# One part of a shared expert's inner layer moved behind the routed experts, and every fetch of their results paced

## The chip, the cores and the metric

The kernel runs on one core of a Trainium2 chip. The metric is the device time of one execution in microseconds (us). PE is the matrix engine (TensorE), DVE the vector engine, ACT the scalar engine with its function tables, POOL the general engine (GpSimd), which here issues the indirect DMAs, and SP the engine that issues most plain DMAs. Lines are written L1367 and so on.

## The reference, cut to what matters

Two blocks with a residual connection each. The first is a two-layer GRU over 1024 tokens of two sequences, and takes some two thirds of the time; the change leaves it alone. The second is a mixture of experts over the 2048 tokens:

```
xf = x.reshape(-1, 256)                                  # 2048 tokens
shared = silu(xf @ w1) * (xf @ w3) @ w2                  # inner width 512
s = sigmoid(concat([xf, t_emb]) @ router_W)              # 8 experts
topk_idx = top_k(s + router_bias, 2)
combine[n, e] = the two chosen s, divided by their sum
h = gelu(einsum('nc,ech->enh', xf, W1e))                 # inner width 256
y = einsum('enh,ehc->enc', h, W2e)
routed = einsum('ne,enc->nc', combine, y)
out = x + (shared + routed) / 3
```

## The kernel before, in words

All is float32. After the GRU the tokens stand in `x1`, 256 features on partitions, and once more by token in `base` and in the DRAM tensor `given`. The function `moe` then does the following.

*Routing.* DVE works out the two experts of each token, their shares, and a sorted order in which each block of 128 slots belongs to one expert. Its product is `pick` (L1179): for each of 39 blocks the tokens to gather. It also makes `words`, the experts' numbers packed eight to a word, which PE's sequencer loads into registers (`owner_of`, L1260), and `slots`, where each token's two results will lie.

*The shared expert's inner layer.* It is cut into 16 parts: four blocks of 512 tokens by four slices of 128 inner features. A part is two accumulated products (`hidden_sums`, L969: w1 into one PSUM bank, w3 into another, each of two 128x512 products; a float32 product shows as two matmul instructions in the profile), a sigmoid on ACT into the buffer `sig` (L981), and two multiplies on DVE, first into `silu` (L982), then into the hidden store (L983). `sig` and `silu` have two buffers each. One part is made before `moe`. Of the other 15, in `parts`, the first `EARLY` are made beside the routing, the next one (up to `FILL`) is spread through the end of the expert loop, and the rest come behind the experts. With EARLY = 8 these are 8, 1 and 6.

*The experts.* `go_through` handles 35 blocks always and up to 4 more under a branch (L1320). A block: POOL gathers 128 token rows from `given` with an indirect DMA (`fetch`, L1274), PE transposes them and DVE copies them (`xT`, L1237 and L1239), PE multiplies by the expert's first weights (`ps_h`, L1245), ACT applies gelu, then transposes, second weights, and a write of y to the DRAM tensor `back` (L1291). Fetches run three blocks ahead.

*Behind the experts.* A part with an order written out by hand, so that each engine gets its instructions just as the Python runs. POOL fetches each token tile's two results from `back` (`fetch_back`, L1335), 32 fetches in all, and DVE adds each times its share onto `base` (`add_gone`, L1349). The first eight fetches (BACK) are issued at once. Then the remaining parts of the inner layer follow, with two fetches behind each part, and then 16 output tiles j with one fetch each while any are left: four accumulated products with w2 into `ps_s` (L1367), an add onto `base` (L1375), and the write of the result from ACT's queue (L1376).

A fetch is paced by a one-element copy on POOL (L1334) from a tile that other work makes to the place that the fetch will fill: the copy can't run before that tile is there, and the fetch can't run before the copy. In the parts the tiles are `sig` and `silu`, in the output tiles `base` of tile j - 1. Before the change, fetches with an even number are paced and those with an odd number follow freely. A PSUM bank comes from one ring of seven (`bank`), so a product waits until DVE or ACT has read what stood in its bank seven allocations earlier.

Of the kernel before, what the change touches and what calls it, by code (L numbers as in the profile page):

```python
# [67 lines left out]

BACK = 8

EARLY = 8
FILL = EARLY + 1


# [935 lines left out]
def moe(ctx, tc, tag, front, out):  # L1010
# [213 lines left out]
    def shared_hidden(parts):  # L1224
        for blk, m in parts:
            pa, pb = (front.hidden_sums(bank, blk, m, name)[0] for name in ("w1", "w3"))
            made = [wk.tile([P, TB], FP, name=name) for name in ("sig", "silu")]
            front.hidden(blk, m, pa, pb, *made)
        return made

    shared_hidden(parts[:EARLY])

# [73 lines left out]

    ((blk, m),) = parts[EARLY:FILL]
    sums = []
# [19 lines left out]
    def fetch_back(behind=None):  # L1328
        i = len(gone)
        if i == 2 * NT:  # L1330
            return
        yb = rows[:, AWAY + i % (ROWS - AWAY), :]
        if behind is not None and i % 2 == 0:
            nc.gpsimd.tensor_copy(yb[0:1, 0:1], behind[0:1, 0:1])  # L1334
        nc.gpsimd.indirect_dma_start(  # L1335
            out=yb,
            out_offset=None,
            in_=back[:, :],
            in_offset=bass.IndirectOffsetOnAxis(ap=slots[:, i % 2, i // 2 : i // 2 + 1], axis=0),
        )  # L1340
        gone.append(yb)
# [14 lines left out]
    with tc.manual_schedule():  # L1356
        for _ in range(BACK):
            fetch_back()
        for i, part in enumerate(parts[FILL:]):
            for made in shared_hidden([part]):  # L1360
                fetch_back(made)
            add_gone(i - 1)
        for j in range(NT):
            fetch_back(base[:, j - 1, :] if j else None)
            ps = bank("ps_s")[:, 0:D]
            for k in range(KS):
                nc.tensor.matmul(  # L1367
                    out=ps,
                    lhsT=front.hid(k, slice(j * P, (j + 1) * P)),
                    rhs=w2_sb[:, k, :],  # L1370
                    start=(k == 0),
                    stop=(k == KS - 1),
                )
            add_gone(min(len(parts[FILL:]) - 1 + j, NT // 2 + j // 2))
            nc.vector.scalar_tensor_tensor(base[:, j, :], ps, 1.0 / 3.0, base[:, j, :], ALU.mult, ALU.add)  # L1375
            nc.scalar.dma_start(out=out[j * P : (j + 1) * P, :], in_=base[:, j, :])  # L1376
# [74 lines left out]
```

## Time and profile before

| | |
|---|---|
| median of three runs | 531.96 us (531.33 to 532.04) |
| the profiled execution | 538.56 us, of it a span of 536.8 us |
| PE busy | 512.1 us, 95% of the span |
| DVE busy | 385.1 us, 72% |
| ACT busy | 243.6 us, 45% |
| POOL busy | 76.9 us, 14% |
| ps_w, 8 early parts and their neighbours | ends at 395.4 us |
| experts | 395.4 to 475 us |
| 6 parts behind the experts | 476.1 to 496.8 us |
| 16 output tiles | 496.8 to 531.2 us |

A row of a timeline gives the start and the duration in us, the engine, the line, the operation, the output and its inputs, how many instructions are merged, and in brackets how long the engine had been idle and what released it. "issue" means that the profile shows nothing that the engine waited for. A row of a line's view gives the shortest, median and longest duration in ns and the first and last start in us; PEldq is PE's sequencer, which runs ahead of the matrix array.

### The profile page before, as it was taken

The page shows a single profiled execution, that of the slowest core. Times are in us where ns is not written, and L with a number is a line of the kernel's source. Part 1 is how long each engine was busy: PE and PEld are TensorE (multiplying, and loading weights), DVE is VectorE, ACT ScalarE, POOL GpSimd, SP SyncE. Part 2 cuts the span into 40 slices and gives each one's busy share as a digit, 9 for nine tenths or more (in the row PEclk, how much of TensorE's full clock was granted, in tenths as well). Part 3 has the DMA queues.
Part 4 walks back from the last instruction along what each step waited for, and adds up shares of the span by engine and source line. Part 5 has one row for each costly group of instructions (what it writes and reads, how often), then busy time and mean ns, then how long its engine had stood idle before and what let it go on. Part 6 is the DMA issues. An engine that isn't in the chain of part 4 may idle for free. (4 is left out here: it accounts for less than half of the span.)

```text
span 536.8 us, 18511 instructions
## 1 busy us (share of the span) xinstructions
PE 512.1 (95%) x7492; PEld 341.2 (64%) x7492; DVE 385.1 (72%) x1296; ACT 243.6 (45%) x833; POOL 76.9 (14%) x124
## 2 busy tenths in 40 slices
PE   7999999999999999999999999989999999999795
PEld 4556766666665545665665666654458888854584
DVE  3665789999888888888888888888953333336372
ACT  3444355655665656656666565641133333341000
POOL 1200000000000000000000000002064444037570
PEclk9999999999999999999999999999999999999888
DMA  8980000000000000000000000001024443223252
GB/s 283 373 259 2 2 3 4 3 4 2 4 32 3 12 1 4 2 23 22 3 23 2 23 22 4 22 21 61 1 88 128 120 125 123 70 72 104 81 177 85
DMA packets 23103, 32.13 MB, mean 60 GB/s; under 512 B 3056, under 2 KB 18544, under 8 KB 22992
## 3 DMA queue, kind: packets, MB, share of 16 engines
q1 hardware_dynamic: 17344, 19.94, 11.0%
q0 software_dynamic: 3216, 8.79, 5.8%
q10 hardware_dynamic: 2448, 2.11, 1.2%
q8 instruction: 63, 1.03, 0.8%
q14 instruction: 32, 0.26, 0.2%
HBM read 21.26 MB, written 9.57 MB: 57 GB/s over the span
## 5 line engine op out<-in xcount | busy, mean ns | idle before, releaser
L296 PE MATMUL ps_step<-whh_sb,h 128*32 128x192 f32 x3616 | 193.3, 331 | 5.4 <-DVE h L369 4.2
L296 PEld LDWEIGHTS ps_step<-whh_sb,h 128*32 128x32 f32 x3616 | 94.6, 109 | 71.4 <-DVE h L369 51.9
L360 DVE TENSOR_TENSOR_SCAN row<-gates,n 128x128 f32<-128x128 f32 x230 | 98.0, 426 | 29.6 <-ACT n L355 28.3
L344 DVE TENSOR_TENSOR_SCAN ps_step<-gates,ps_step 128x128 f32<-128x128 f32 x230 | 97.3, 423 | 15.0 <-ACT gates L341 15.0
L268 PE MATMUL ps_step<-wih_sb,h 128*32 128x192 f32 x1696 | 99.7, 328 | 4.1 <-ACT ps_step L526 2.4
L355 ACT ACTIVATE n<-ps_step 128x64 f32<-128x64 f32 x228 | 53.0, 232 | 111.0 <-DVE ps_step L344 110.9
L341 ACT ACTIVATE gates<-ps_step 128x128 f32<-128x128 f32 x230 | 66.5, 289 | 35.5 <-PE ps_step L296 26.0
L268 PEld LDWEIGHTS ps_step<-wih_sb,h 128*32 128x32 f32 x1696 | 57.4, 110 | 26.8 <-ACT ps_step L526 14.5
L369 DVE STREAM_TRANSPOSE h<-row 128x64 f32<-128x64 f32 x230 | 56.5, 246 | 8.0
L969 PE MATMUL ps_w<-x_sb,w_sb 128*128 128x512 f32 x128 | 57.3, 597 | 0.2 <-PEq L1320 0.2
L268 PE MATMUL ps_in<-wih_sb,h 128*32 128x192 f32 x1024 | 54.4, 328 | 1.8 <-ACT h L257 1.4
L1239 DVE COPY hT<-ps_hT 128x256 f32<-128x256 f32 x35 | 14.9, 425 | 49.0 <-PE ps_hT L1237 47.1
L526 ACT COPY ps_step<-inputs 128x256 f32<-128x256 f32 x123 | 47.8, 389 | 0.0
L357 DVE SCALAR_TENSOR_TENSOR n<-gates,row 128x64 f32<-128x64 f32 x224 | 47.0, 210 | 0.0
L268 PEld LDWEIGHTS ps_in<-wih_sb,h 128*32 128x32 f32 x1024 | 34.0, 110 | 14.6 <-issue 4.6
L526 ACT COPY ps_step<-bt 128x256 f32<-128x256 f32 x106 | 39.9, 376 | 3.3
L1274 POOL DMA_INDIRECT inputs<-given,pick x35 | 33.3, 951 | 55.2 <-PE ps_xT L1237 31.9
L969 PEld LDWEIGHTS ps_w<-x_sb,w_sb 128*128 128x128 f32 x128 | 23.6, 190 | 27.1 <-issue 24.7
L1245 PE MATMUL ps_h<-w1e_sb,xT 128*128 x140 | 36.1, 380 | 0.7 <-DVE xT L1239 0.7
L1245 PE MATMUL ps_y<-w2e_sb,hT 128*128 x140 | 36.0, 380 | 0.0
L1335 POOL DMA_INDIRECT inputs<-back,slots x32 | 30.9, 964 | 30.0 <-issue 28.3
L1245 PEld LDWEIGHTS ps_y<-w2e_sb,hT 128*128 128x128 f32 x140 | 26.4, 190 | 4.8 <-DVE hT L1239 1.3
(179 smaller groups left out, 430.9 us busy)
## 6 DMA issues: line engine op xcount, KB each, us to landing
back<-y SPq DMA_DIRECT2D x35, 128.0 KB
w1e_sb<-in_w1e SPq DMA_DIRECT2D x1, 2048.0 KB
w2e_sb<-in_w2e SPq DMA_DIRECT2D x1, 2048.0 KB
given<-inputs SPq DMA_DIRECT2D x8, 256.0 KB
out_dram<-inputs ACTq DMA_DIRECT2D x16, 128.0 KB
whh_sb<-in_whh SPq DMA_DIRECT2D x2, 768.0 KB
x_sb<-in_xT SPq DMA_DIRECT2D x3, 512.0 KB
w_sb<-in_w SPq DMA_DIRECT2D x3, 512.0 KB
```

Source lines behind the costliest of these rows:

```text
L268: last = nc.tensor.matmul(out=out[cols(q), :, :], lhsT=given(k), rhs=self.wih[layer][:, k, q * 3 * U : (q + 1) * 3 * U].rearrange("p (g u) ...
L296: nc.tensor.matmul(out=by_sum(self.sums[layer])[cols(q), 0:3, :], lhsT=self.states[layer][:, k, :], rhs=self.whh[layer][:, k, q * 3 * U : ...
L341: nc.scalar.activation(gates[:, :, :, 1], sums[:, 1:3, :], AF.Sigmoid)
L344: nc.vector.tensor_tensor_scan(s, gates[:, 0, :, :].rearrange("p u i -> p (u i)"), ps[:, 0 : 6 * U : 3], 0.0, ALU.mult, ALU.add,)
L355: nc.scalar.activation(n[:, :, 0], s[:, 1 : 2 * U : 2], AF.Tanh, scale=-1.0 if keep is None else keep)
L357: nc.vector.scalar_tensor_tensor(n[:, :, 1], gates[:, 1, :, 1], 1.0, h, ALU.subtract, ALU.mult)
L360: nc.vector.tensor_tensor_scan(row.rearrange("p u i -> p (u i)"), gates[:, 1, :, :].rearrange("p u i -> p (u i)"), n.rearrange("p u i -> p ...
L369: nc.vector.transpose(to, row)
L526: return nc.scalar.copy(by_sum(banks[layer][tick % 2])[:, 0:4, :], g.sum_bias[1] if layer else inputs[:, group_of(0, tick), :, :],)
L969: last = self.tc.nc.tensor.matmul(out=ps, lhsT=self.later[name][:, k, m * P : (m + 1) * P], rhs=self.x1[:, k, blk * TB : (blk + 1) * TB], ...
L1245: nc.tensor.matmul(out=ps, lhsT=of[:, k, :], rhs=weights_sb[:, bass.ds(e * KD + k, 1), :], start=(k == 0), stop=(k == KD - 1),)
L1274: nc.gpsimd.indirect_dma_start(out=xg, out_offset=None, in_=given[:, :], in_offset=bass.IndirectOffsetOnAxis(ap=pick[:, i : i + 1], axis=0),)
```

## The change

EARLY goes from 8 to 7. So 7 parts are made beside the routing, the part in the expert loop's end is the eighth of `parts` (block 2, slice 0) and no longer the ninth (block 2, slice 1), and 7 parts come behind the experts. With two fetches behind each, 22 of the 32 fetches are issued before the output tiles and not 20. In `fetch_back` the condition on even numbers is gone, so that every fetch is paced that is given a tile: 14 in the parts and 9 in the output tiles.

```
-EARLY = 8
+EARLY = 7
 FILL = EARLY + 1
...
         yb = rows[:, AWAY + i % (ROWS - AWAY), :]
-        if behind is not None and i % 2 == 0:
+        if behind is not None:
             nc.gpsimd.tensor_copy(yb[0:1, 0:1], behind[0:1, 0:1])
         nc.gpsimd.indirect_dma_start(
             out=yb,
```

More of the change, by code (lines that the diff above doesn't have):

```diff
@@ L69 @@
 BACK = 8
-EARLY = 8
+EARLY = 7
 FILL = EARLY + 1
@@ L1332, in fetch_back @@
         yb = rows[:, AWAY + i % (ROWS - AWAY), :]
-        if behind is not None and i % 2 == 0:
+        if behind is not None:
             nc.gpsimd.tensor_copy(yb[0:1, 0:1], behind[0:1, 0:1])
```

## Prediction

> **What bounds the kernel now.** I read the page first (busy shares, the chain that ended last), then the timeline of PE, POOL, ACT and DVE from 360 us on, then PE's sequencer at the lines where the experts begin. All times are of the one profiled execution.
>
> ```profile
> PE 512.1 (95%) x7492; PEld 341.2 (64%) x7492; DVE 385.1 (72%) x1296; ACT 243.6 (45%) x833; POOL 76.9 (14%) x124
> PE ps_s L1367 6%; PE ps_w L969 4%; DVE inputs L1375 0%
> ```
> PE is the bound, and from 476 us to the end its own instructions are the chain. The change leaves the first 365 us alone (the recurrent layers, L296 and L268).
>
> Where the experts begin, PE's timeline:
> ```profile
> 387.61 7.97 PE L969 MATMUL ps_w<-x_sb,w_sb 128*128 128x512 f32 x18
> 395.42 0.60 PE L1237 MATMUL ps_xT<-ident,inputs 128*128 128x128 f32 x4
> 396.70 1.13 PE L1245 MATMUL ps_h<-w1e_sb,xT 128*128 x4 [0.68 <-DVE xT L1239]
> ```
> A part of the inner layer is 8 of these matmuls. The 18 are the tail of the sixth early part, the seventh and the eighth; the eighth is the one that moves. PE looks full right up to the first expert, so one would think that all of its time comes back. The sequencer's instructions say otherwise:
> ```profile
> L1237 PEldq EVENT_SEMAPHORE  x2: 51/51/51, 392.6 to 392.9; - x2
> L1260 PEldq TENSOR_LOAD <-words x1: 493/493/493, 393.5 to 393.5; - x1
> L1245 PEldq EVENT_SEMAPHORE  x1: 51/51/51, 394.3 to 394.3; - x1
> ```
> The waits for the first two gathers pass at 392.6 and 392.9, then the experts' numbers are loaded at 393.5, and the first expert's product is ready to go out at 394.35. This is hidden now because the matrix array has queued work until 395.4.
>
> POOL, at the two places where it gathers:
> ```profile
> 388.55 1.18 POOL L1274 DMA_INDIRECT inputs<-given,pick  x1 [19.99 <-DVE pick L1179]
> 390.03 0.94 POOL L1274 DMA_INDIRECT inputs<-given,pick  x1 [0.31 <-issue]
> ...
> 487.36 0.18 POOL L1334 COPY inputs<-sig 1x1 f32<-1x1 f32 x1
> 487.80 0.97 POOL L1335 DMA_INDIRECT inputs<-back,slots  x1 [0.27 <-POOL inputs L1334]
> 489.08 0.95 POOL L1335 DMA_INDIRECT inputs<-back,slots  x1 [0.30 <-issue]
> 490.04 0.18 POOL L1334 COPY inputs<-sig 1x1 f32<-1x1 f32 x1
> ...
> 510.38 0.36 POOL L1334 COPY inputs<-inputs 1x1 f32<-1x1 f32 x1 [3.87 <-DVE inputs L1375]
> 511.08 1.00 POOL L1335 DMA_INDIRECT inputs<-back,slots  x1 [0.33 <-POOL inputs L1334]
> ```
> A pair with one copy takes 490.04 - 487.36 = 2.68 us, an unpaced fetch 1.25 us, so a paced one 1.43 us. POOL never waits here before 506 us.
>
> The chain of waits at the end:
> ```profile
> 476.11 20.84 PE ps_w L969 x48
> 496.95 6.26 PE ps_s L1367 x29
> 503.21 0.46 issue
> ...
> 507.90 23.23 PE ps_s L1367 x94
> ```
> Six parts take 20.7 us (3.44 each). The 128 products of ps_s begin at 496.79 and at their steady 0.216 us would take 27.6 us, to 524.4; they end at 531.1. So 6.7 us are lost between 503 and 514, to gaps that no instruction explains and then to half clock. The execution took 538.56 us, 6.60 over the median of 531.96. I read this stall as that one execution's and not the timed runs' (an estimate, from 6.7 against 6.6). The sum below is a difference and is put on both.
>
> **The change part by part.**
> *Taken from the front:* 8 weight loads and 8 matmuls (8 x 0.43 = 3.44 us of PE), one sigmoid on ACT (0.60), two multiplies on DVE (2 x 0.69), no DMA. PE then ends the seventh part at 391.99 instead of 395.42. But the first gather starts only when DVE has made `pick` (388.25), which the change does not hasten. So the transposes go out at 392.65 and 393.05; DVE, free at 392.88, copies the first until 393.55; and the sequencer, having passed the second gather's wait at 392.95, still takes its 1.4 us to 394.35 for the load of the experts' numbers. The first product starts at about 394.45 instead of 396.69: 2.24 us earlier, not 3.44. Behind it gathers keep ahead of their use (the sixth starts at 395.03, freed by the earlier transposes, and is wanted near 401), and the gelu table load on ACT comes 3.4 us earlier too.
>
> *A rule against the row.* The first gather took 392.6 - 388.55 = 4.05 us from its issue, the second 2.9. The Trainium skill, "DMA: Bandwidth & Descriptors", section "Anatomy of one DMA — SWDGE (gpsimd) path", gives about 2.0 us plus bytes over 436 GB/s, so 2.3 us for 128 KB. By the rule the gather lands at 390.85, the sequencer has its numbers before PE is free, and the front gives back all 3.44: sum 0. By the row it gives 2.24. I take the row.
>
> *Added behind:* the same 3.44 us of PE after the branch at L1320, where PE has no gap to take it: +3.44. Nothing of SP's or POOL's queue comes with it, apart from two fetches that now run in the part loop and not in the output loop. The part in the middle of the experts' end (FILL) becomes (2,0) instead of (2,1), the same work.
>
> *Pacing:* copies go from 11 to 23, each 0.18 us and its hand-over, 1.43 - 1.25 = 0.18 us of POOL: 2.1 us on POOL in all. Queued behind each copy are all later fetches. New too: a silu buffer (two of them) is free only when POOL has copied from it, so DVE's multiply two parts on waits for POOL, with L983 and the adds behind it. Counted from the first part's first matmul (POOL's first fetch is at +1.54, as 477.65 - 476.11): the eight free fetches end at 11.25, the copies then come every 1.43; those of parts 3 and 4 end at 20.0 to 24.3, and let parts 5 and 6 be finished on DVE at 22.8 and 25.6. PE wants the bank of the last part again at 34.5 (ps_s tile 6), so it does not wait. The last fetch ends at 11.25 + 23 x 1.43 + 1.25 = 45.4; with 2.0 to land and 1.0 for two adds, 48.4, and the last add stands before the output multiply of tile 14, whose sums are ready at 24.1 + 15 x 1.73 = 50.0. Hidden, with 1.6 us to spare; the cover is PE's 27.6 us of ps_s.
>
> Sum: -2.24 + 3.44 + 0 = +1.20 us. On the median: 533.2. On the profiled execution: 539.8 with the stall, 533.1 without.
>
> *A second rule, against the change.* From 392.0 to 394.45 PE would have only four transposes. The Trainium skill, "TensorE: Matmul & The Clock Gate", section "Part 1: The HAM clock gate (the "warmup" mystery)", has the clock halved after an idle window of about 3.4 us; an opening of 2.4 us would then cost nothing. This trace is stricter: the clock went to half at 506.66 after a stretch of 3.4 us in which PE still ran five matmuls of 0.216 us, 32% of it. The worst stretch of that length at the front would hold about 0.4 us of the seventh part, 0.44 of transposes and 0.55 of ps_h, 40%. Half clock cost 2.8 us there (14 matmuls in 5.79 us instead of 3.02). By the rule the sum stays +1.20, by the row it could be +4.0. I take 0, since 40% is over 32%, and keep 2.8 as the high end.
>
> **The rivals.**
> *A. No change (531.9 to 532.5).* The gather lands sooner in the timed runs, or the number load overlaps more. For it: the rule above, and the array's queue is full in the profile. Against: both waits passed exactly as the gathers' traffic ended (DMA share 0.73 at 392.0 to 392.4). It decides if the first product starts before 393.8, 0.6 us sooner than I say.
>
> *B. POOL becomes the bound (534.0 to 537.8).* The limit for a paced fetch is (50.0 - 15.5)/23 = 1.50 us. Two copies behind DVE's output cost 0.70 us to the fetch (510.38 to 511.08), not 0.44. If the nine in the output loop do, 2.4 us come, less 1.6 to spare: +2.0 in all. If all 23 do, 6.2 - 1.6 + 1.2 = +5.8. Against: later copies of that loop took 0.18 again.
>
> *C. Faster (525 to 531).* If the stall at 503 us is in the timed runs too and fetches cause it, spacing them ends it: up to -6.7 + 1.2 = -5.5. Against: POOL issues without pause in both, so 1.43 instead of 1.34 us a fetch is hardly thinner traffic, and the 6.6 us argue that the timed runs lack it. It decides if over 2.3 us of a real stall go.
>
> **How the numbers follow.** The three runs lie within 0.13%, so about 0.2% (1.06 us) can be told from no change. Likeliest, 0.58: 533.2, own range 532.6 to 533.9; of it 0.44 lies beyond 1.06 us and 0.14 within. A has 0.09, B 0.13, the half clock (536.0) 0.07, C 0.13. So slower 0.44 + 0.13 + 0.07 = 0.64, same 0.14 + 0.09 = 0.23, faster 0.13. The range 530.5 to 536.3 leaves out most of C and the far end of B.
>
> **What would show it.** Right: PE's last ps_w before the experts ends near 392.0; xT at 392.7; first ps_h near 394.4 with some 2 us of idle around it; 56 ps_w after the branch; copies of sig and silu 14, of base 9; the part loop 24 us without PE gaps. Wrong: ps_h before 393.8 (A); the last L1375 waiting for a fetch, or paced fetches over 1.5 us apart (B); ps_s without gaps in the timed runs, and a gain (C).

## The result and the profile after

The changed kernel took 532.47 us in the median (532.05 to 534.17, 14 runs), the kernel before 531.59 us (14 runs). The ratio of the means is 1.0022, with a 95% interval of 1.0013 to 1.0030: 1.2 us slower (0.7 to 1.6), where the sum said +1.20. The medians lie 0.9 us apart. The profiled execution took 532.48 us, of it a span of 530.7.

The page after, busy shares:

```profile
PE 509.8 (96%) x7492; PEld 340.6 (64%) x7492; DVE 385.2 (73%) x1296; ACT 243.5 (46%) x833; POOL 79.5 (15%) x136
```
POOL has its twelve copies more (136 instructions, not 124). That PE's busy time is 2.3 us lower than on the page before is no gain of the change: the half clock of that first execution is missing from it.

PE's timeline where the experts begin, and below it PE's sequencer at the same place (shortest, median, longest in ns, then first and last start in us):

```profile
387.09 4.54 PE L969 MATMUL ps_w<-x_sb,w_sb 128*128 128x512 f32 x10
392.18 0.77 PE L1237 MATMUL ps_xT<-ident,inputs 128*128 128x128 f32 x4 [0.55 <-DMA inputs<-given,pick]
393.91 1.10 PE L1245 MATMUL ps_h<-w1e_sb,xT 128*128 x4 [0.96 <-DVE xT L1239]
```
```profile
L1237 PEldq EVENT_SEMAPHORE  x2: 51/51/51, 392.1 to 392.4; - x2
L1260 PEldq TENSOR_LOAD <-words x1: 492/492/492, 393.0 to 393.0; - x1
L1245 PEldq EVENT_SEMAPHORE  x1: 51/51/51, 393.8 to 393.8; - x1
```
Everything stands 0.52 us earlier in this trace, `pick` at 387.54, so times are best counted from `pick`. The seventh part now ends first, PE waits for the gather and then once more, and ps_h starts at pick + 6.37. Before it was pick + 8.63. The bracket blames DVE's copy of xT for the second wait. But DVE copied the two blocks' xT from 392.62 to 393.41, and the first block's copy, the only one that this product needs, was done well ahead of 393.91. What ended just before ps_h is the load of the experts' numbers and what the sequencer does behind it.

The chain of waits at the end:

```profile
473.10 24.27 PE ps_w L969 x56
497.37 27.64 PE ps_s L1367 x128
525.01 0.02 issue
525.04 0.42 DVE inputs L1375
```
Seven parts now take 24.27 us, and ps_s takes the 27.6 us that it should. No stall is there.

A second profile of the unchanged kernel:

> The kernel before, unchanged, for a second profile. My theory: the 6.7 us lost between 503 and 514 us in the first profile were that execution's own, so here the 128 products of ps_s take 27.6 us without a break, the last output add comes about 136.4 us behind the pick, and the span is near 530 us. Rival (the stall belongs to the kernel): ps_s takes some 34 us again and the span is near 537 us.

It took 531.41 us with a span of 529.6. Its chain:

```profile
475.62 20.84 PE ps_w L969 x48
496.46 27.64 PE ps_s L1367 x128
524.10 0.02 issue
524.12 0.42 DVE inputs L1375
```
The stall was the first execution's own. With this trace (`pick` at 387.77, ps_h at pick + 8.62) the whole difference can be counted from `pick` to the last output add, which comes at +136.35 before and at +137.50 after: ps_h comes 2.25 us sooner; from there to the first part behind the experts 79.22 and 79.19 us go by, so 0.03 sooner; the parts take 24.27 in place of 20.84, so 3.43 later; ps_s takes the same. That is 1.15 us later in all.

### The profile page after: what moved, and what is told of

It is laid out like the page before. It is cut to its first block, busy times and chain, and to the rows that moved or that the text cites. A ratio compares the mean times of both kernels' runs of the same rounds, so it can differ in the third digit from the quotient of the medians.

```text
span 530.7 us, 18536 instructions
## 1 busy us (share of the span) xinstructions
PE 509.8 (96%) x7492; PEld 340.6 (64%) x7492; DVE 385.2 (73%) x1296; ACT 243.5 (46%) x833; POOL 79.5 (15%) x136
## 5 line engine op out<-in xcount | busy, mean ns | idle before, releaser
L1285 ACT ACTIVATE he<-ps_h 128x256 f32<-128x256 f32 x35 | 13.4, 383 | 35.3 <-PE ps_h L1245 35.3
```

## The experiments

**Only the part moved.** On the kernel before, pacing as it was:

```
-EARLY = 8
+EARLY = 7
```


> EARLY = 7 with fetches paced as before (every second one). My theory: the move alone costs what the change costs, because PE gets 3.44 us more behind the experts and only some 2.25 us back in front: +1.2 us, ratio about 1.0022. In the profile ps_h stands 6.4 us after pick, as in the changed kernel, against 8.6 before. The rival that pacing is the cost: ratio 1.000. POOL is under less load than in the changed kernel, so its last fetch lands earlier, near 519.5 where the changed kernel has 521.8.

Measured 532.64 us, ratio 1.0013 (1.0004 to 1.0022); ps_h at pick + 6.20, last output add at pick + 137.32. The move alone brings the loss. Its interval overlaps with that of the whole change, so by the times the extra pacing cannot be told from nothing when the part has moved. The traces say more: from ps_h to the last output add 131.13 us go by in this kernel and in the changed one. What differs between the two, 0.17 us, lies ahead of ps_h, where the gathers' waits passed 0.1 to 0.2 us sooner here.

**Only the pacing.** On the kernel before, EARLY still 8:

```
-        if behind is not None and i % 2 == 0:
+        if behind is not None:
```


> EARLY = 8, every fetch paced. The prediction called pacing free, with the moved part's 3.44 us as cover. By the changed kernel's rows the last fetch lands 48.7 us after the first part's first matmul, two adds take 1.06 and two output adds 0.7, while PE without the moved part ends at 48.3 us: so here POOL should be the bound and the kernel some 2 us slower, ratio about 1.004. If pacing is free by itself: 1.000. If it helps: below 1.000.

Measured 534.6 us (5 runs), ratio 1.0051 (1.0037 to 1.0065): slower than the whole change, by itself. PE's front is as before (ps_h at pick + 8.63). DVE near the end, and then the last drains of POOL's and SP's queues:

```profile
521.14 0.48 DVE L1349 SCALAR_TENSOR_TENSOR inputs<-inputs,share 128x256 f32<-128x256 f32 x1 [0.80 <-DMA inputs<-back,slots]
...
523.78 1.07 DVE L1349 SCALAR_TENSOR_TENSOR inputs<-inputs,share 128x256 f32<-128x256 f32 x2 [1.50 <-DMA inputs<-back,slots]
```
```profile
L770 POOLq INC_SWDGE_SEM  x1: 1501/1501/1501, 524.5 to 524.5; - x1
L1445 POOLq DRAIN  x3: 40/107/5549, 526.0 to 532.2; - x3
L1445 SPq DRAIN  x3: 7/7/13, 529.7 to 531.9; - x3
```
The adds now wait for fetches, and the last output add comes at pick + 137.63, 1.28 us later than before. And behind the last fetch POOL has 1.50 us and then a drain of 5.55 us, from 526.04 to 531.59, while SP, which waits for the last output, reaches its own at 529.7. So POOL ends the program, some 1.9 us after SP. From POOL's first fetch to its last 44.2 us go by, against 41.2 in the second profile of before: 3.0 us for 12 copies, 0.25 us each. The loss of 2.7 us is more than the 2 us expected, since POOL's end was not in that sum. So the pacing is not free by itself; in the changed kernel it is the moved part that hides it.

**One part more moved,** on the changed kernel:

```
-EARLY = 7
+EARLY = 6
```


> EARLY = 6, every fetch paced: a second part goes behind. If the experts' start hangs on pick, the gather and the load of the experts' numbers, the front gives nothing more back: ps_h still 6.4 us after pick, +3.44 us on the changed kernel, +4.6 in all, ratio 1.0087. If the front gave back a fixed share of each part (65%): +2.4, ratio 1.0045. PE would be idle for some 4 us ahead of the transposes; by the rule of a 3.4 us idle window the clock halves there and up to 2.8 us come on top (ratio up to 1.014).

Measured 539.61 us, ratio 1.0145 (1.0130 to 1.0161). PE where the experts begin, and a table by stretch (length; PE, weight loads, DVE, ACT and POOL busy, each with its instructions; granted clock; DMA share and GB/s):

```profile
386.94 1.10 PE L969 MATMUL ps_w<-x_sb,w_sb 128*128 128x512 f32 x2
391.72 1.17 PE L1237 MATMUL ps_xT<-ident,inputs 128*128 128x128 f32 x4 [3.68 <-DMA inputs<-given,pick]
393.65 2.05 PE L1245 MATMUL ps_h<-w1e_sb,xT 128*128 x4 [0.75 <-DVE xT L1239]
```
```profile
390.24:397.06 6.82, 4.59 (x13) 3.37 (x14) 1.62 (x4) 0.38 (x1) 4.99 (x7) 0.50 0.37 107
397.06:403.00 5.94, 5.94 (x35) 5.22 (x35) 2.27 (x6) 1.89 (x5) 3.09 (x4) 1.00 0.38 110
```
ps_h stands at pick + 6.25 (`pick` at 387.40), no sooner than with EARLY = 7: the front has nothing more to give. On top of it PE idles 3.7 us, the clock is halved from 390.24 for 6.8 us, and the first ps_h take 2.05 us in place of 1.10. (The 3.4 us window in the expectation is that of the prediction's second rule.) The last output add comes 6.26 us later after the pick than with the change. PE behind the experts shows that the half clock is only a part of it:

```profile
472.49 1.88 PE L969 MATMUL ps_w<-x_sb,w_sb 128*128 128x512 f32 x4
475.80 1.52 PE L969 MATMUL ps_w<-x_sb,w_sb 128*128 128x512 f32 x3 [1.43 <-DVEq L1320]
```
The parts take 27.70 and not 24.27 us, so the second part costs its whole 3.43. From ps_h to the last ps_w ahead of the branch (472.49 here, 471.07 in the changed kernel) 78.84 us go by and not 77.16: 1.68 us for the half clock, of whose 6.8 us the last 3.4 fall behind the start of ps_h. From there to the first part behind the branch it is 3.31 and not 2.03 us, because that part now waits for DVE at the branch (L1320): 1.28 us, which the expectation lacks. That the time met the highest ratio of the expectation, 1.014, is therefore luck: 1.68 and 1.28 us together come near the 2.8 us that were put on the half clock alone. The wait for DVE comes back below.

**A second copy in each paced fetch,** on the changed kernel:

```
             nc.gpsimd.tensor_copy(yb[0:1, 0:1], behind[0:1, 0:1])
+            nc.gpsimd.tensor_copy(yb[0:1, 1:2], behind[0:1, 1:2])
```


> The changed kernel with two pacing copies for each paced fetch (a second element from the same tile). 23 more copies of 0.18 to 0.25 us put 4.1 to 5.8 us on POOL. By the changed kernel's rows the last fetch can be some 1.65 us later before the end moves. So my theory: 2.5 to 4.1 us slower than the changed kernel, ratio to before 1.007 to 1.010. If POOL is the bound already: 4.1 to 5.8 us slower, ratio 1.010 to 1.013. If POOL has room that I don't see: no change, 1.0022.

Measured 535.1 us (5 runs), ratio 1.0055 (1.0042 to 1.0069), 1.75 us above the changed kernel by the two ratios. POOL's timeline (its lines stand one lower here), and the drains:

```profile
521.44 0.18 POOL L1334 COPY inputs<-inputs 1x1 f32<-1x1 f32 x1
521.57 0.17 POOL L1335 COPY inputs<-inputs 1x1 f32<-1x1 f32 x1
522.01 0.98 POOL L1336 DMA_INDIRECT inputs<-back,slots  x1 [0.27 <-POOL inputs L1335]
```
```profile
L1446 POOLq DRAIN  x3: 40/107/5549, 527.0 to 533.1; - x3
L1446 SPq DRAIN  x3: 7/7/13, 530.8 to 532.8; - x3
```
The second copy starts 0.13 us after the first, so 23 of them are 3.0 us on POOL (first fetch to last: 46.8 us against 43.7), less than the 4.1 to 5.8 us expected. Of the 3.0 us 1.75 shows, which is under the 2.5 to 4.1 us expected. Once more POOL's drain, to 532.50, ends the program, 1.7 us after SP's first one at 530.8. So of the pacing's cover some 1.3 us had been left, and here it is used up.

**Where the front's missing 1.2 us lie.** First the changed kernel without the load of the first experts' numbers. Its first eight blocks take the first expert's weights by a constant, so it leaves out the choice of expert for them, and with it the register work behind the load:

```
-                rhs=weights_sb[:, bass.ds(e * KD + k, 1), :],
+                rhs=weights_sb[:, k : k + 1, :] if e is None else weights_sb[:, bass.ds(e * KD + k, 1), :],
...
+        if i < IDS:
+            return None
...
```


> The changed kernel, with the first eight blocks always multiplied by the first expert's weights (addressed by a constant), so that PE's sequencer loads no expert numbers before the ninth block; gathers stay as they are. My theory: ps_h follows the pick by 6.37 us in the changed kernel because the sequencer loads the numbers behind the second gather's wait; without that load the first product waits only for DVE's copy of xT, which ends near pick + 5.5, so ps_h starts at about pick + 5.55, the front gives back 3.1 of 3.44 us and the kernel is at about 1.0007 of the one before (+0.4 us). Rival (the gather alone sets the start, the load is hidden behind it): ps_h stays at pick + 6.2 to 6.4 and the ratio at 1.0022.

Measured 531.86 us, ratio 1.0004 (0.9996 to 1.0012). `pick` stands at 387.30:

```profile
391.63 0.87 PE L1237 MATMUL ps_xT<-ident,inputs 128*128 128x128 f32 x4 [0.26 <-DMA inputs<-given,pick]
392.56 1.13 PE L1245 MATMUL ps_h<-w1e_sb,xT 128*128 128x256 f32 x4
```
ps_h starts at pick + 5.26, 1.11 us sooner than in the changed kernel's trace. Of that some 0.2 us are the gathers, whose waits passed a little sooner here (pick + 4.23 and 4.69, not 4.53 and 4.89); in the kernel with the second copy they passed at 4.24 and 4.69, and there ps_h came at pick + 6.19. So the load costs 0.93 us at equal gathers, and by the ratio, which falls by 0.0018, 0.96 us. In the four traces in which the load is exposed, ps_h follows the start of the load by 0.92 to 0.97 us, whenever the gathers landed. So nearly all that the front held back was the load.

Then, in addition, plain loads of rows 0 to 255 for the first two blocks, which leaves out the choice of their tokens:

```
+        if i < 2:
+            nc.sync.dma_start(out=xg, in_=given[i * P : (i + 1) * P, :])
+        else:
...
```


> As the kernel without the load of numbers, and the first two blocks take their rows by two plain loads of given (rows 0 to 255) on SP's queue instead of the two gathers, so that nothing at the front waits for the pick but the third block. My theory: PE then goes from the seventh part straight on to the transposes and to ps_h at about pick + 5.2 or sooner, the front gives back all of the 3.44 us that it lost, and the kernel stands at 1.000 of the one before (within 0.3 us). If the front had given back all that PE was freed of already, and the 1.2 us came from behind the experts (pacing), it would stay at 1.0022.

Measured 531.39 us, ratio 0.9997 (0.9989 to 1.0005), ps_h at pick + 5.19 (`pick` at 388.54):

```profile
388.08 4.54 PE L969 MATMUL ps_w<-x_sb,w_sb 128*128 128x512 f32 x10
392.45 0.60 PE L1237 MATMUL ps_xT<-ident,inputs 128*128 128x128 f32 x4
393.73 1.13 PE L1245 MATMUL ps_h<-w1e_sb,xT 128*128 128x256 f32 x4 [0.68 <-DVE xT L1239]
```
No gap ahead of the transposes is left, 3.43 us come back, and the kernel stands where the one before does. The two intervals of this pair overlap, so the gathers' own share beyond the load is too small to be told; 0.07 us by the traces. Nothing of the 1.2 us is left for the pacing. But little more could have been had with POOL paced like this: its last drain now ends at SP's or behind it, 0.05 us behind in the trace without the load and 0.9 us in this one.

**The gap that the kernel before has, filled.** In the kernel before, PE idles 0.68 us ahead of ps_h for DVE's copy of xT, in both of its traces. Here the eighth early part is written by hand around the first two blocks' transposes, the pacing is that of before, and `go_through` skips the two fetches already made:

```
-    shared_hidden(parts[:EARLY])
+    shared_hidden(parts[: EARLY - 1])
...
+    with tc.manual_schedule():
...
+        pa = front.hidden_sums(bank, blk7, m7, "w1")[0]
+        fetch(0)
+        fetch(1)
+        pb = front.hidden_sums(bank, blk7, m7, "w3")[0]
+        front.hidden(blk7, m7, pa, pb, *(wk.tile([P, TB], FP, name=name) for name in ("sig", "silu")))
     go_through(0, SURE, (begin_part, go_on))
```


> The kernel before with its pacing and its eight early parts, but the eighth cut in two by hand: its w1 product, then the fetches and transposes of the first two blocks, then its w3 product, so that PE has 1.72 us of work between the first transposes and ps_h. My theory: in the kernel before PE idles 0.68 us ahead of ps_h for DVE's copy of xT; with w3 there the copy is hidden, ps_h starts at pick + 8.0 instead of pick + 8.64, and the kernel is at about 0.999 of the one before (-0.5 to -0.6 us). Rival (PE waits for the gathers ahead of w3 in its queue, so the idle time only moves): ratio 1.000 or up to +0.3 us.

Measured 532.1 us, ratio 1.0009 (1.0001 to 1.0017): the wrong side. ps_h did come sooner, at pick + 7.79 (`pick` at 387.61), by 0.83 us. PE around the branch behind the experts:

```profile
472.49 1.88 PE L969 MATMUL ps_w<-x_sb,w_sb 128*128 128x512 f32 x4
475.80 1.52 PE L969 MATMUL ps_w<-x_sb,w_sb 128*128 128x512 f32 x3 [1.43 <-DVEq L1327]
```
```profile
L1326 DVEq TENSOR_LOAD <-slots_taken x1: 544/544/544, 474.8 to 474.8; - x1
L1327 DVEq COMPARE_BRANCH  x1: 72/72/72, 475.4 to 475.4; - x1
L1327 DVEq EVENT_SEMAPHORE  x1: 21/21/21, 475.6 to 475.6; - x1
```
The first product behind the branch now waits for DVE, whose sequencer first loads the number of slots and takes the branch (here L1326 and L1327). It is the wait that EARLY = 6 showed. In the kernel before, that product's weight load waits for ACT alone (second profile):

```profile
475.59 0.30 PEld L969 LDWEIGHTS ps_w<-x_sb,w_sb 128*128 128x128 f32 x2 [0.95 <-ACTq L1320]
```
The reason is the PSUM bank. In the programs as they are built, the bank that this product gets was last used under the branch by a transpose, which DVE copies, both here and with EARLY = 6; before and after the change it was last used by a product that ACT reads. So DVE has to pass the branch first. (Behind the branch the bank is not strictly the one of seven allocations earlier: the order in which banks come free under the branch decides.)

**The same, with the ring turned.** One bank more is taken ahead of the split part, and DVE writes one element of it (0.06 us). Only what is added to the split kernel is marked:

```
     with tc.manual_schedule():
...
+        for _ in range(1):
+            nc.vector.memset(bank("ps_pad")[0:1, 0:1], 0.0)
         pa = front.hidden_sums(bank, blk7, m7, "w1")[0]
```


> The kernel with the eighth early part split, and one PSUM bank more taken from the ring ahead of it (DVE sets one element of it to 0), so that the first product behind the experts falls on a bank that ACT and not DVE read last, as in the kernel before. In the split kernel ps_h came 0.83 us sooner after the pick, but the first part behind the branch waited 1.43 us on DVE's sequencer (its load of slots_taken and its branch). My theory: without that wait the 0.83 us are kept: ps_h at pick + 7.8, first part behind the experts at ps_h + 79.2, last output add at pick + 135.5 to 135.7, ratio to the kernel before 0.9984 to 0.9990 (-0.5 to -0.85 us). Rival (the split itself costs the time, for instance by a later start of the following gathers or by the pace of the experts): first part behind at ps_h + 80.4 again and a ratio of 1.0005 to 1.0012.

Measured 530.56 us (529.64 to 531.29, 12 runs) against 531.62 for the kernel before, ratio 0.9978 (0.9970 to 0.9987). This version beats both kernels. PE at the front (`pick` at 387.23), at the branch, and the chain at the end:

```profile
392.87 0.60 PE L1237 MATMUL ps_xT<-ident,inputs 128*128 128x128 f32 x4
393.30 1.88 PE L969 MATMUL ps_w<-x_sb,w_sb 128*128 128x512 f32 x4
395.02 1.03 PE L1245 MATMUL ps_h<-w1e_sb,xT 128*128 x4
```
```profile
472.11 1.88 PE L969 MATMUL ps_w<-x_sb,w_sb 128*128 128x512 f32 x4
474.14 3.24 PE L969 MATMUL ps_w<-x_sb,w_sb 128*128 128x512 f32 x7
```
```profile
474.14 20.84 PE ps_w L969 x48
494.97 27.64 PE ps_s L1376 x128
522.62 0.02 issue
522.64 0.42 DVE inputs L1384
```
The w3 product fills the gap, ps_h follows it without idle time at pick + 7.80, the first part behind starts 79.1 us later and not 80.4, and the last output add comes at pick + 135.41, 0.93 us sooner than before, a little more than expected. One bank more is the only difference to the split kernel, and the wait for DVE is gone. So the rival, that the split itself costs the time, is out.

## Why the prediction was right, and where it was not

- *The whole:* +1.20 us was forecast as a difference, and +1.2 was measured. The 533.2 us that were put on the median came out as 532.47, just outside the narrow range of 532.6 to 533.9, because the three runs of before that it was added to were 0.4 us above the median of 14.
- *Taken from the front, -2.24:* measured -2.25. The chain was read rightly: gather's wait, load of the numbers, first product. That the two agree to 0.01 us is chance: ps_h stands at pick + 6.20 and 6.19 in two other traces with EARLY = 7, which is -2.4, because the gathers' waits passed sooner there. The first gather was issued at 388.03 and its wait passed at 392.1, again 4.1 us (3.7 to 4.1 in all the traces that have it), so the row holds here and not the 2.3 us estimated from the Trainium skill, "DMA: Bandwidth & Descriptors", section "Anatomy of one DMA — SWDGE (gpsimd) path". The run without the load sharpens it: the late gather matters because the load stands behind it. Without the load, the gathers let the front give back 3.36 of 3.44 us.
- *Added behind, +3.44:* measured +3.43, with nothing of PE idle in it.
- *Pacing, 0:* right in the sum, wrong in its margin. It holds only together with the moved part, which pushes ps_s 3.4 us back behind POOL's fetches and lets 22 fetches go ahead of it. Alone, the same pacing cost about 2.7 us. The term that was mis-sized is the "1.6 us to spare". In the changed kernel's trace:

```profile
518.33 0.98 POOL L1335 DMA_INDIRECT inputs<-back,slots  x1 [0.27 <-POOL inputs L1334]
```
```profile
521.93 1.06 DVE L1349 SCALAR_TENSOR_TENSOR inputs<-inputs,share 128x256 f32<-128x256 f32 x2
523.31 0.42 DVE L1375 SCALAR_TENSOR_TENSOR inputs<-ps_s,inputs 128x256 f32<-128x256 f32 x1 [0.32 <-PE ps_s L1367]
525.04 0.42 DVE L1375 SCALAR_TENSOR_TENSOR inputs<-ps_s,inputs 128x256 f32<-128x256 f32 x1 [1.30 <-PE ps_s L1367]
```
  The last fetch's adds end 0.3 us ahead of the output add of tile 14. Landing took 3.5 us from the issue (518.33 to 521.84), where the sum had 1.25 and 2.0, and the last issue came at 43.7 us after POOL's first, where the sum had 42.6: beside the parts paced fetches came 1.47 us apart and not 1.43. The prediction also left out POOL's own end: the last landing is followed by 1.50 and 5.55 us on POOL, and in this trace that ends 0.8 us before SP is done (529.08 to 529.85). (POOL did wait once before 506 us, 0.15 us for a sigmoid at 500.9; the sum does not hang on it.)
- *The stall read as one execution's:* right. Neither the second profile of before nor that of after has it.
- *Half clock, 0:* right for this change; the granted clock stays whole where the experts begin. The comparison of 40% with 32% counted matmuls at 0.216 us. By PE's busy column it is 1.89 of 3.4 us (56%) in the emptiest stretch of the changed kernel against 1.54 (45%) ahead of the stall's half clock, so the margin was wider than thought. The high end of 2.8 us is not confirmed: with EARLY = 6 the half clock cost 1.7 us.
- *silu waits for POOL, PE does not:* right:

```profile
485.95 0.69 DVE L982 TENSOR_TENSOR silu<-ps_w,sig 128x512 f32<-128x512 f32 x1 [4.08 <-POOL inputs L1334]
```
  DVE waited 6.3 us in all for POOL's copies from `silu`, while the chain shows PE's parts without a break.
- *Rivals:* A (no change) needed ps_h before 393.8; counted with the shift of 0.52 us, that is 393.3, and it came at 393.9. B (POOL the bound) did not happen, but one copy more per fetch, or the part not moved, brings it about, with 1.75 and 2.7 us. C fell with the stall. The median of 532.47 us lies in A's range, but the front moved as the sum said, and so it is not A.

Still open: by the times, the move alone and the whole change differ by less than their intervals, so a pacing cost of a few tenths either way is not excluded; one trace of each, with 131.13 us from ps_h to the last output add in both, speaks for none. Whether a faster gather with the load kept would give the front back was not tried.

## What to carry to other kernels

Before work is moved out of a busy stretch, read the sequencer's own instructions at the next stage: what the freed engine then waits for can be a chain that the removed work had hidden, here a gather and a register load behind it, while the moved work is paid in full at its new place. Slack of an engine off the path has to be counted to the end of the program, with what the engine does behind its last transfer. When one edit in a ring of buffers moves another stage, look at which engine read the buffer last; shifting the ring by one buffer can be worth more than the edit. And when a forecast is met in sum, add up its parts from the trace: with EARLY = 6 two different costs filled the place of one.

## What the runs showed of the hardware

- The load of eight experts' numbers takes the sequencer 0.49 us. With the register work behind it, ps_h starts 0.92 to 0.97 us after the load does, and without the load it came 0.93 us sooner at equal gathers.
- With EARLY = 6 the granted clock was halved at 390.24, only 2.2 us into a PE idle stretch of 3.68 us (from 388.04), and stayed so for 6.83 us. In the stalled execution of before it was halved at 506.66, for 6.83 us too. By PE's busy column the 3.4 us ahead held 1.20 us of work (35%) and 1.54 us (45%), so PE had not been idle throughout. In the changed kernel, with its two gaps of 0.55 and 0.96 us, the emptiest 3.4 us held 1.89 us (56%), and the clock stayed whole. Where between them the limit lies was not measured.
- The price of the half clock was what PE had to do in those 6.83 us: 1.7 us where ps_h began halfway through, 2.8 us in the stall (14 matmuls in 5.79 us and not 3.02).
- A one-element copy ahead of a fetch costs POOL 0.25 us in all without the moved part (44.2 against 41.2 us for 12 copies) and 0.14 us with it (43.7 against 42.0 us in the run with the part alone moved); a second copy right behind the first costs 0.13 us.
- Behind the last fetched row POOL needs 7.05 us to the end of its queue, 5.55 of them one drain. This was the same within 0.01 us in ten of the eleven traces; in the run with plain loads it was 6.85 us.
- Where a product had to wait until DVE had passed a branch, PE was idle for 1.43 us (two kernels). DVE's sequencer took 0.54 us to load the number that decides the branch and 0.07 us for the branch itself.
